# A graph layer with a routed expert layer: idle writes in the counting, a later attention, and a divided last piece

## The chip, the cores and the metric

The kernel runs on one core of a Trainium2 chip. The metric is the device time of one execution in microseconds (us); the time before is the median of three runs. Engines are named as in the profile: PE (TensorE; PEld its weight loads), DVE (VectorE), ACT (ScalarE), POOL (GpSimd) and SP, which issues most plain DMAs. GpSimd issues the indirect DMAs: gathers of rows by an index column, and scatters.

## The reference, cut to what matters

x is [128 graphs, 128 nodes, 256], adj is [128, 128, 128]; M = 16384 nodes.

```python
x = x + gnn(layernorm(x), adj)      # (1+eps) x + adj @ x, then a 256-512-256 MLP with relu
xn = layernorm(x)
h = xn @ W_gat                      # 16 values a node: 4 heads x 4 experts
# 1048576 edges (src, dst) and a loop on every node: softmax over the edges of each dst
e = leaky_relu(a_src[src] + a_dst[dst], 0.2)
alpha = softmax of e over the edges with the same dst
agg = segment_sum(h[src] * alpha, dst)
scores = layernorm(agg).mean over heads      # 4 scores a node
w, i = softmax(top_2(scores))
x = x + sum over the two chosen experts: w * (gelu(xn @ W1[i] + b1[i]) @ W2[i] + b2[i])
```

JAX clips or wraps edge indices, so edges whose source lies outside the range count too: they all take the last row, and only their number by destination matters. The kernel calls finding that number the counting.

## The kernel before, in words

**First stage (to about 680 us).** The graph layer runs tile by tile (32 tiles of four graphs); VectorE sorts the real edges beside it (`sort_edges`). Each node's 24 attention values go to `table` in DRAM, the normalized rows and the residual of the first 88 graphs to `xr`, the turned rows to `xn_d`.

**Second stage, in an order written out by a planner.** Class `Plan` holds lists of Python generators for three engines ("pool", "tensor", "vector"). A task issues some instructions and yields what they are thought to cost, or a condition: `plan.was(name)` waits until something is `done`, `plan.after(us)` until so much planned time is over. The planner always steps the engine that is free first, so these costs decide in which order the instructions of each engine stand. On the chip each engine runs its own list in that order and waits for real data.

- *Counting* (`count_edges`, class `Runs`, L489 to L773): a sorting network over 8192 int16 numbers a partition. A step is one VectorE instruction of at most 2048 pairs (`_cuts`, L509), with its cost yielded; `_pairs` is L496, `build` L520, `merge` L538, `push` L652. Then `histogram` (L700) counts with matmuls (L745, closed by L760): VectorE makes the operands (L727, L737), TensorE multiplies between its expert matmuls.
- *Gathers* (`Gathers.task`, L909, issued at L873): 13 blocks of 47 columns, each column one indirect DMA of 128 rows of `table` into `hs`; the last block is one plain load from `last`, which `last_block` (L985) packs. `pitch` (L899) is the planned time of one: 1.6 beside the counting, 1.33 after. Up to three blocks (and two of the blocks 3, 4, 8) may be ahead of attention. Rows asked for with `ask` (piece results `fin`, routed rows `r_x`, scatters at L880) go between them. A small copy `seen<-marks` (L864) ties GpSimd to TensorE's progress.
- *Attention* (`attend`, L1051): per block a segmented softmax by scans on VectorE (L1085 to L1140), with exponentials on ScalarE (L1121), and a store of running states. Ahead of it `spread` (L952) places destination values, and `last_block` waits for one gathered row `e` (L1030, L1032) and moves it by matmuls (L1041).
- *Pieces* (`pieces`, L2188): the graphs in seven pieces (ends 32, 52, 64, 82, 88, 106, 128); when the states of a piece are there, its ends are gathered (`fin`), and `finish_attention` and `gates` (L1154, L1218) make the weights.
- *Dense experts* (class `Experts`, L1547, L1566): for the last 40 graphs (tiles 22 to 31) all four experts are computed, 40 units, stored to `ys`, and added with their gates later (`stored`, L2245, additions at L2272) when the piece's gates are known. In the built program a unit is 8 L1547, 2 L1560 and 16 L1566; the profile counts each twice.
- *Routed experts* (`Routes`, `Routed`): the first 88 graphs are routed. After five pieces a list (`Routes.task`) sorts nodes into units of 256 nodes for one pair of experts; 47 units. A unit gathers its rows (`r_x`, two DMAs), is turned by TensorE (`turn`, L1693) and copied by ScalarE (L1697), multiplied (L1712, L1566), finished on VectorE (L1735 with the bias, L1745 with the result), and scattered to the output (L880). Seven row buffers: the rows of unit u + 7 are asked for when unit u has been scattered.

Of the kernel before, what the change touches and what calls it, by code (L numbers as in the profile page):

```python
# [13 lines left out]
F32 = mybir.dt.float32  # L14
# [11 lines left out]
P = 128  # L26
# [39 lines left out]
BARE_US = 6.95  # L66
TURN_US = 0.8
GATHER_US = 1.33
BESIDE_US = 1.6
LAND_US = 4.0  # L70
AHEAD_US = 6.0
SCALAR_US = 4.0
LOCK_US = 0.02
# [4 lines left out]
AHEAD = (3, 4, 8)  # L78
AHEAD_BUFS = 2
HIST_US = 2.0  # L80
SLACK_US = 20.0
PART = 3
YIELD_US = 16.0
# [10 lines left out]
    for start, (stop, a, b) in zip([0] + [g for g, _, _ in PARTS], PARTS)  # L94
]
PIECES = [slice(a, b) for a, b in zip(
    (0, 32, 52, 64, 82, 88, 106), (32, 52, 64, 82, 88, 106, 128)
)]
MOST = 32
EARLY = 4  # L100
# [388 lines left out]
class Runs:  # L489

    def __init__(self, nc, a, b, length, n):
        self.nc, self.pair, self.length, self.n = nc, Pair(a, b), length, n

    def _pairs(self, d):  # L496

        nc, s = self.nc, self.n // self.length
        v = self.pair.cur[:, 0 : self.n].rearrange("p (k t d) -> p k t d", t=2, d=d * s)
        o = self.pair.other[:, 0 : self.n].rearrange("p (k t d) -> p k t d", t=2, d=d * s)  # L500
        for t, op in enumerate((ALU.max, ALU.min)):
            for cols, cost in self._cuts(self.n // 2, d * s):
                nc.vector.tensor_tensor(
                    o[:, :, t, cols], v[:, :, 0, cols], v[:, :, 1, cols], op=op
                )
                yield cost
        self.pair.swap()

    def _cuts(self, n, inner):  # L509
# [10 lines left out]
    def build(self):  # L520

        nc, n, s = self.nc, self.n, self.n // self.length
        run = 1
        while run < self.length:
            v = self.pair.cur[:, 0:n].rearrange("p (k t l s) -> p k t l s", t=2, l=run, s=s)
            o = self.pair.other[:, 0:n].rearrange("p (k t l s) -> p k t l s", t=2, l=run, s=s)
            a, b = v[:, :, 0, :, :], v[:, :, 1, ::-1, :]
            for t, op in enumerate((ALU.max, ALU.min)):
                for cols, cost in self._cuts(n // 2, s):
                    nc.vector.tensor_tensor(  # L530
                        o[:, :, t, :, cols], a[..., cols], b[..., cols], op=op
                    )
                    yield cost
            self.pair.swap()
            yield from self._clean(run // 2)
            run *= 2

    def merge(self, keep_all):  # L538

        nc, n, s = self.nc, self.n, self.n // self.length  # L540
        v = self.pair.cur[:, 0:n].rearrange("p (l t s) -> p l t s", t=2, s=s // 2)
        a, b = v[:, :, 0, :], v[:, ::-1, 1, :]
        out = self.pair.other
        for at, op in ((0, ALU.max), (n // 2, ALU.min))[0 : 2 if keep_all else 1]:
            half = out[:, at : at + n // 2].rearrange("p (l s) -> p l s", s=s // 2)
            for cols, cost in self._cuts(n // 2, s // 2):
                nc.vector.tensor_tensor(half[:, :, cols], a[:, :, cols], b[:, :, cols], op=op)
                yield cost
        if keep_all:
            d = self.length // 2  # L550
            self.pair.swap()

            self.length *= 2
            yield from self._clean(d)
        else:
            self.n //= 2
            self.pair.swap()
            yield from self._clean(self.length // 2)
# [13 lines left out]
def count_edges(tc, nc, c, sp, dram):  # L572

    raw = [c.counted_raw] + [sp.tile([P, 4096], I32, name=f"raw{i}") for i in range(2)]
    pick = picks(nc, sp)
    runs = Runs(nc, c.counted, raw[1].bitcast(I16), 32, EC)
    yield from runs.build()
    yield from runs.merge(False)
    yield from runs.to_one()
    if runs.pair.cur is not c.counted:  # L580
        raw = [raw[1], raw[0], raw[2]]
    lst = runs.pair.cur[:, 0:CROW]
    col = c.col


    far_op, small = CROW / 960 + 0.15, CROW / 1920 + 0.15
    nz = raw[1][:, 0:CROW].bitcast(F32)
    nc.vector.tensor_single_scalar(nz, lst, 0.0, op=ALU.is_gt)
    yield small

    NONE = 2 * CROW * P
    empty = raw[0][:, CROW // 2 : CROW].bitcast(BF16)
    nc.vector.tensor_scalar(
        empty, lst, 0.0, float(NONE), op0=ALU.is_equal, op1=ALU.mult
    )
    yield small
    dst = raw[2][:, 0:CROW]
    nc.vector.tensor_scalar(dst, lst, -1.0, float(M), op0=ALU.mult, op1=ALU.add)
    yield small
    cbk = raw[2][:, CROW:]  # L600
    nc.vector.tensor_single_scalar(cbk, dst, 7, op=ALU.arith_shift_right)
    yield small
    nc.vector.tensor_single_scalar(dst, dst, P - 1, op=ALU.bitwise_and)
    yield small
    at = raw[1][:, CROW:].bitcast(F32)
    nc.vector.memset(at[:, 0:1], 0.0)
    for lo, hi in ((1, CROW // 2), (CROW // 2, CROW)):
        nc.vector.tensor_tensor(
            at[:, lo:hi], cbk[:, lo:hi], cbk[:, lo - 1 : hi - 1], op=ALU.not_equal
        )  # L610
        yield far_op / 2
    for v in halves(CROW):
        nc.vector.tensor_tensor(at[:, v], at[:, v], col[:, v], op=ALU.mult)
        yield far_op / 2
    first = raw[0][:, CROW:].bitcast(F32)
    for v in halves(CROW, 4):
        nc.vector.tensor_tensor_scan(
            first[:, v], at[:, v], at[:, v],
            first[:, v.start - 1 : v.start] if v.start else 0.0, op0=ALU.max, op1=ALU.max,
        )  # L620
        yield far_op / 2
    for v in halves(CROW):
        nc.vector.tensor_tensor(at[:, v], col[:, v], first[:, v], op=ALU.subtract)
        yield far_op / 2
    nc.vector.scalar_tensor_tensor(
        at, at, float(CKC), nz, op0=ALU.is_ge, op1=ALU.mult, accum_out=c.bad[:, 7:8]
    )
    yield far_op
    for v in halves(CROW):
        nc.vector.scalar_tensor_tensor(  # L630
            first[:, v], cbk[:, v], float(CKC), first[:, v], op0=ALU.mult, op1=ALU.subtract
        )
        yield far_op / 2
    low = dst.bitcast(F32)
    for v in halves(CROW):
        nc.vector.scalar_tensor_tensor(
            low[:, v], first[:, v], float(P), dst[:, v], op0=ALU.mult, op1=ALU.add
        )
        yield far_op / 2
    value, moved = raw[1], raw[2]  # L640
    for v in halves(CROW):
        nc.vector.tensor_tensor(value[:, v], low[:, v], empty[:, v], op=ALU.max)
        yield far_op / 2


    nc.vector.tensor_single_scalar(
        value[:, CROW:], value[:, 0:CROW], P * CROW, op=ALU.bitwise_xor
    )
    yield small
    w = P * CKC  # L650

    def push(value, moved, by, rate):  # L652
        for v in halves(w, 2 if rate == 1 else 1):
            nc.vector.tensor_single_scalar(
                moved[:, v], value[:, v], P * by, op=ALU.bitwise_xor
            )
            yield w / 1920 / 2 + 0.1
        for v in halves(w - by, 4 // rate):
            to = slice(v.start + by, v.stop + by)
            nc.vector.tensor_tensor(value[:, to], moved[:, v], value[:, to], op=ALU.min)  # L660
            yield (w - by) / 960 / 4 + 0.1

    by = CROW // 2
    while by >= P:
        yield from push(value, moved, by, 1)
        by //= 2
    both = raw[0].bitcast(I16)
    value, moved = both[:, 0:w], both[:, w:]
    for v in halves(w, 4):
        nc.vector.tensor_single_scalar(value[:, v], raw[1][:, v], P * P, op=ALU.min)  # L670
        yield w / 960 / 4
    while by:
        yield from push(value, moved, by, 2)
        by //= 2
    yield from histogram(nc, c, value, raw, pick, sp)
# [167 lines left out]
class Gathers:  # L843
# [53 lines left out]
        return pool.tile([P, CB, ROW], F32, name="hs")  # L897

    def pitch(self):  # L899
        return GATHER_US if "counts" in self.plan.at else BESIDE_US  # L900

    def ask(self, todo, name, how=None, soon=False):
# [82 lines left out]
def last_block(nc, c, plan, gathers, once, ps):  # L985
# [42 lines left out]
    gathers.ask([(row, gathers.table, source)], "last row")  # L1028
    yield 1.5
    yield plan.was("last row")  # L1030
    each = once.tile([P, CB * ROW], F32, name="room")
    nc.vector.tensor_tensor(  # L1032
        each.rearrange("p (c f) -> p c f", f=ROW),
# [17 lines left out]
def attend(nc, c, plan, gathers, states, dst_t, aw, once, ps, ahead):  # L1051
# [2 lines left out]
    dst_x = aw.tile([P, H, COLS], F32, name="dst_x")  # L1054
    nc.gpsimd.memset(dst_x[:, :, 0 : COLS - P], 0.0)
    yield from spread(nc, c, dst_t, dst_x, once)
    yield from last_block(nc, c, plan, gathers, once, ps)
    pre_ex = [once.tile([P, 2, H, CB + 1], F32, name=f"pre{i}") for i in range(2)]
    for t in pre_ex:
# [1 line left out]
    before = None  # L1061
    for k in range(NBL):
        if k >= EARLY:
            yield plan.was("counts")
        yield plan.was(f"block{k}")
        hs = gathers.rows.pop(k)
        cols = slice(k * CB, (k + 1) * CB)
# [702 lines left out]
def adj_ffn_kernel(  # L1770
# [352 lines left out]
    with tc.tile_pool(name="moe", bufs=2) as mp, tc.tile_pool(  # L2123
# [98 lines left out]
        def lists(routes):  # L2222
# [7 lines left out]
            for k, reach in enumerate(REACH):  # L2230
# [3 lines left out]
                experts.routed = routed  # L2234
                experts.ask()
                plan.done("listed", 5.0)
            plan.done("routes")

        def sums():
# [448 lines left out]
```

## Time and profile before

| what | value |
|---|---|
| runs | 2069.66, 2071.39, 2074.95 us; median 2071.39 |
| profiled execution, own time | 2072.77 us |
| its span (first to last instruction) | 2071.0 us |
| mean granted TensorE clock | 0.973 |
| PE busy | 1926.6 us, 93% |
| DVE busy | 1553.8 us, 75% |
| POOL busy | 1115.6 us, 54% |
| gathers `hs` (L873) | 564, mean 1.13 us |

How to read it: busy time is the union of an engine's instructions. Idle time is put down to what ended it, "issue" where nothing that the profile shows did. The waits list an engine and its line, what it waited for, the sum in us, how often, and the longest. A timeline row is start, length, engine, line, operation, output<-inputs and shape; equal neighbours are merged (x4).

### The profile page before, as it was taken

What the parts mean: (1) busy time and instruction counts of PE and PEld (TensorE: products, weight loads), DVE (VectorE), ACT (ScalarE), POOL (GpSimd) and SP (SyncE); (2) the same over time, 40 slices, a digit from 0 to 9 for tenths busy, and PEclk for the clock granted to TensorE, in tenths of its full rate; (3) what the DMA queues carried; (4) which work ended last, traced back from release to release, by engine and by line L of the source; (5) the groups of instructions that cost most, each with busy time, mean ns of one, the idle gap of its engine ahead of it and who ended that gap; (6) DMA issues with size and microseconds to landing.
All of it is one profiled execution on the core that took longest, in us unless ns stands there. A gap on an engine that the chain in (4) does not pass through costs nothing. (4 is left out here: it accounts for less than half of the span.)

```text
span 2071.0 us, 28612 instructions
## 1 busy us (share of the span) xinstructions
PE 1926.6 (93%) x8938; PEld 1443.0 (70%) x8938; DVE 1553.8 (75%) x4106; ACT 854.1 (41%) x1541; POOL 1115.6 (54%) x1064
## 2 busy tenths in 40 slices
PE   7999989889999799999999999999899999999894
PEld 4666767657666465666667666888788787788783
DVE  5889999858898797999983653747636856858576
ACT  5878544444443222333232433344334343335241
POOL 2111111111110688888877777777777767774723
PEclk9999999999999899999999999999999999999997
DMA  9888888697762121233213444444564355666955
GB/s 238 213 230 210 193 243 193 179 188 179 121 140 75 57 58 49 60 131 100 69 41 113 123 144 126 104 143 135 183 209 136 97 178 139 147 149 216 369 177 199
DMA packets 299157, 313.38 MB, mean 151 GB/s; under 512 B 111649, under 2 KB 239603, under 8 KB 298870
## 3 DMA queue, kind: packets, MB, share of 16 engines
q1 hardware_dynamic: 231382, 241.19, 36.8%
q0 software_dynamic: 67616, 70.28, 19.3%
q8 instruction: 75, 1.23, 0.2%
q14 instruction: 84, 0.69, 0.1%
HBM read 156.93 MB, written 130.32 MB: 139 GB/s over the span
## 5 line engine op out<-in xcount | busy, mean ns | idle before, releaser
L873 POOL DMA_INDIRECT hs<-table,index x564 | 637.6, 1130 | 165.1 <-issue 154.5
L1566 PE MATMUL big<-mw,m_hid 128*128 (+1 forms) x2784 | 626.2, 382 | 0.0
L1566 PEld LDWEIGHTS big<-mw,m_hid 128*128 128x128 f32 x2784 | 522.2, 190 | 84.6 <-issue 17.0
L1712 PE MATMUL m_phid<-m_xn,mw 128*128 128x256 f32 x1504 | 344.7, 386 | 27.9 <-ACT m_xn L1697 21.7
L1712 PEld LDWEIGHTS m_phid<-m_xn,mw 128*128 128x128 f32 x1504 | 285.8, 192 | 71.9 <-ACT m_xn L1697 26.0
L1573 ACT COPY m_out<-big 128x1024 f32<-128x1024 f32 x87 | 88.1, 1012 | 528.3 <-PE big L1566 522.5
L1547 PE MATMUL m_phid<-m_xn,mw 128*128 128x512 f32 x640 | 288.1, 601 | 10.6 <-issue 10.0
L1965 POOL DMA_DIRECT2D at<-in_adj_dram x31 | 41.4, 1334 | 433.7 <-DMA at<-self_eye 368.3
L2047 PE MATMUL big<-w_sb,hid 128*128 128x256 f32 x1024 | 237.9, 388 | 11.1 <-ACT h_t L2028 10.7
L2036 PE MATMUL p_hid<-h_t,w_sb 128*128 128x512 f32 x512 | 232.3, 604 | 9.6 <-ACT h_t L2028 7.2
L2047 PEld LDWEIGHTS big<-w_sb,hid 128*128 128x128 f32 x1024 | 194.3, 194 | 42.0 <-ACT h_t L2028 16.7
L1547 PEld LDWEIGHTS m_phid<-m_xn,mw 128*128 128x128 f32 x640 | 121.8, 192 | 145.3 <-issue 131.2
L1718 ACT ACTIVATE m_hid<-m_phid,r_b 128x256 f32<-128x256 f32 x376 | 155.9, 472 | 153.0 <-PE m_phid L1712 115.6
L2036 PEld LDWEIGHTS p_hid<-h_t,w_sb 128*128 128x128 f32 x512 | 94.7, 192 | 118.1 <-issue 97.8
L1551 ACT ACTIVATE m_hid<-m_phid,mb 128x512 f32<-128x512 f32 x160 | 108.7, 687 | 141.3 <-PE m_phid L1547 141.2
L873 POOL DMA_INDIRECT fin<-states,ends x128 | 142.9, 1116 | 37.5 <-issue 33.4
L1745 DVE SCALAR_TENSOR_TENSOR r_x<-m_out,r_x 128x256 f32<-128x256 f32 x188 | 87.1, 484 | 61.3 <-ACT m_out L1573 53.0
L880 POOL DMA_INDIRECT out_dram<-r_x,places x94 | 110.5, 1175 | 28.6 <-issue 12.3
L873 POOL DMA_INDIRECT r_x<-xr,nodes x94 | 99.9, 1063 | 36.6 <-issue 24.6
L2040 ACT ACTIVATE hid<-p_hid,b_sb 128x512 f32<-128x512 f32 x128 | 87.2, 682 | 77.1 <-PE p_hid L2036 77.1
L2019 POOL DMA_DIRECT2D xt<-b_sb x32 | 43.2, 1351 | 106.2 <-ACT xn L1903 63.5
L1735 DVE SCALAR_TENSOR_TENSOR r_x<-b_rows,r_x 128x256 f32<-128x256 f32 x188 | 87.2, 485 | 6.3 <-issue 2.2
(393 smaller groups left out, 2520.5 us busy)
## 6 DMA issues: line engine op xcount, KB each, us to landing
mw<-in_L_ffn_W_dram SPq DMA_DIRECT2D x102, 512.0 KB
states<-room SPq DMA_DIRECT2D x55, 564.0 KB
ys<-m_out SPq DMA_DIRECT2D x40, 512.0 KB
y_in<-ys SPq DMA_DIRECT2D x40, 512.0 KB
xt<-in_x_dram SPq DMA_DIRECT2D x32, 512.0 KB
xt<-b_sb POOLq DMA_DIRECT2D x32, 512.0 KB
x_d<-x SPq DMA_DIRECT2D x32, 512.0 KB
xn_d<-xn_t SPq DMA_DIRECT2D x32, 512.0 KB
```

What stands on the lines that cost most here:

```text
L873: self.nc.gpsimd.indirect_dma_start(out=out, out_offset=None, in_=rows, in_offset=bass.IndirectOffsetOnAxis(ap=index, axis=0),)
L880: sc = self.nc.gpsimd.indirect_dma_start(out=rows, out_offset=bass.IndirectOffsetOnAxis(ap=index, axis=0), in_=values, in_offset=None, bou ...
L1547: nc.tensor.matmul(p_hid, w1[:, k, f * P : (f + 1) * P], xn[:, k, :], start=(k == 0), stop=(k == 1),)
L1551: nc.scalar.activation(hid[:, f, :], p_hid, AF.Gelu, bias=b1[:, f : f + 1])
L1566: nc.tensor.matmul(p_y[:, s, :], hid[:, f, s * P : (s + 1) * P], w2[s // 2][:, f, :], start=(f == 0 and not b2), stop=(f == DH // P - 1 an ...
L1573: nc.scalar.copy(y, p_y)
L1712: nc.tensor.matmul(p_hid[:, half], w1[i][:, k, f * P : (f + 1) * P], xt[:, k, :], start=(k == 0), stop=(k == 1),)
L1718: nc.scalar.activation(hid[:, f, half], p_hid[:, half], AF.Gelu, bias=b1[i][:, f : f + 1])
L1735: self.nc.vector.scalar_tensor_tensor(x[:, s, D : 2 * D], b2[i], x[:, s, 2 * D + i : 2 * D + i + 1], x[:, s, D : 2 * D], op0=ALU.mult, op1 ...
L2036: nc.tensor.matmul(p_hid, w1_sb[:, k, f * P : (f + 1) * P], h_t[:, k, :], start=(k == 0), stop=(k == 1),)
L2040: nc.scalar.activation(hid[:, f, :], p_hid, AF.Relu, bias=b1_sb[:, f : f + 1])
L2047: nc.tensor.matmul(p_y[:, s, :], hid[:, f, s * P : (s + 1) * P], w2_sb[:, f, :], start=(f == 0), stop=(f == DH // P - 1),)
```

## The change

Behind every counting step whose planned cost is at least 1.0, VectorE writes zeros over 230 float32 numbers of a tile `pad` that nobody reads (`rest`); 156 such writes are built. Attention blocks from number 4 (the fifth) on wait for the first list, and no longer for the counting. The last piece (graphs 106 to 128) is two, 106 to 117 and 117 to 128. The work behind the gathered row `e` in `last_block` comes 20 planned us later. The planned pitch of a gather is 1.8 until `spread` is over, then 1.36 beside the counting instead of 1.6; since the planner orders by these costs, the order on every engine of the second stage changes with them.

```diff
-BESIDE_US = 1.6
+SPREAD_US = 1.8
+BESIDE_US = 1.36
+LAST_US = 20.0
+REST = 230
+REST_US = 0.11
 PIECES = [slice(a, b) for a, b in zip(
-    (0, 32, 52, 64, 82, 88, 106), (32, 52, 64, 82, 88, 106, 128)
+    (0, 32, 52, 64, 82, 88, 106, 117), (32, 52, 64, 82, 88, 106, 117, 128)
 )]
...
+    def rest(self, cost):
+        if cost < 1.0:
+            return cost
+        self.nc.vector.memset(self.pad, 0.0)
+        return cost + REST_US
...   (in _pairs, build and merge)
-                yield cost
+                yield self.rest(cost)
...   (count_edges)
+    pad = sp.tile([P, REST], F32, name="pad")
...   (push)
-            yield w / 1920 / 2 + 0.1
+            yield runs.rest(w / 1920 / 2 + 0.1)
-            yield (w - by) / 960 / 4 + 0.1
+            yield runs.rest((w - by) / 960 / 4 + 0.1)
...   (pitch)
+        if "spread" not in self.plan.at:
+            return SPREAD_US
...   (last_block)
     yield plan.was("last row")
+    yield plan.after(LAST_US)
...   (attend)
     yield from spread(nc, c, dst_t, dst_x, once)
+    plan.done("spread")
...
         if k >= EARLY:
-            yield plan.was("counts")
+            yield plan.was("first list")
...   (lists, after each list)
                 plan.done("listed", 5.0)
+                plan.done("first list")
```

More of the change, by code (lines that the diff above doesn't have):

```diff
@@ L489, with __init__ @@
 class Runs:
-    def __init__(self, nc, a, b, length, n):
+    def __init__(self, nc, a, b, length, n, pad):
         self.nc, self.pair, self.length, self.n = nc, Pair(a, b), length, n
+        self.pad = pad
+    def rest(self, cost):
[3 more added lines that the diff above has]
+        return cost + REST_US
     def _pairs(self, d):
@@ L532, in build @@
                     )
-                    yield cost
+                    yield self.rest(cost)
             self.pair.swap()
@@ L547, in merge @@
                 nc.vector.tensor_tensor(half[:, :, cols], a[:, :, cols], b[:, :, cols], op=op)
-                yield cost
+                yield self.rest(cost)
         if keep_all:
@@ L575, in count_edges @@
     pick = picks(nc, sp)
-    runs = Runs(nc, c.counted, raw[1].bitcast(I16), 32, EC)
+    pad = sp.tile([P, REST], F32, name="pad")
+    runs = Runs(nc, c.counted, raw[1].bitcast(I16), 32, EC, pad)
     yield from runs.build()
```

## The prediction

> **What bounds the kernel now.** I read the page first, then the granted clock and busy time in stretches of 100 us, then the waits of TensorE, then the timelines of single engines where these pointed. The first 680 us (graph layer, edge sort) are the same instructions in both programs except for eight idle writes near the end, so only the rest matters.
>
> ```profile
> span 2071.0 us, 28612 instructions
> PE 1926.6 (93%) x8938; PEld 1443.0 (70%) x8938; DVE 1553.8 (75%) x4106; ACT 854.1 (41%) x1541; POOL 1115.6 (54%) x1064
> ```
>
> TensorE is busy nearly throughout, so time can come only from its holes and from what follows its last matmul. The timeline of the end (start, length, both in us; the bracket is the idle time before):
>
> ```profile
> 2040.08 1.01 ACT L1573 COPY m_out<-big 128x1024 f32<-128x1024 f32 x1 [5.85 <-issue]
> 2041.12 1.92 DVE L1745 SCALAR_TENSOR_TENSOR r_x<-m_out,r_x 128x256 f32<-128x256 f32 x4
> 2042.96 15.92 DVE L2272 SCALAR_TENSOR_TENSOR acc<-y_in,gate,acc 128x256 f32<-128x256 f32 x40
> 2046.58 13.15 POOL L880 DMA_INDIRECT out_dram<-r_x,places  x1 [0.30 <-DVE acc L2272]
> ```
>
> TensorE's last row there is 13.98 us from 2026.02, so it ends at 2040.0. Then 10 of the 40 dense additions (L2272, four instructions each) still stand on VectorE until 2058.9, and the last scatter of GpSimd, which needs 1.0 to 1.3 us elsewhere, lies under them for 13.15 us. It ends at 2059.74, and the closing takes 11.3 us more. The waits of TensorE (us in total, times, longest):
>
> ```profile
> PE big L1693 <- DMA r_x<-xr,nodes: 8.7, 5, 3.1
> PE pt L1041 <- DVE room L1032: 2.9, 1, 2.9
> PE big L745 <- DVE counted L737: 2.6, 1, 2.6
> ```
>
> and, on VectorE, the wait behind the second of these:
>
> ```profile
> DVE room L1032 <- DMA e<-table,e: 16.4, 1, 16.4
> ```
>
> The r_x line is the important one: routed rows come through GpSimd, which issues 881 indirect transfers. An undisturbed one takes 0.95 us and 0.30 of issue, 1.26 in all, which reads as 76% busy: the stretches from 700 to 1800 show 73 to 84%, so GpSimd is full there. Beside the counting it is slower. Two rows of its timeline, both beside 2048-wide L503 steps (1.22 us each):
>
> ```profile
> 818.86 0.95 POOL L873 DMA_INDIRECT hs<-table,index  x1 [0.30 <-issue]
> 821.37 1.97 POOL L873 DMA_INDIRECT hs<-table,index  x1 [0.30 <-issue]
> ```
>
> Some gathers meet the seam between two steps and pass, others wait a whole step. Adding up both timelines from 684.5 to 1116.3: the stretches of long steps hold 106 gathers in 192.2 us, 1.81 each. Outside them: 17 in 33.7 us (spread), 89 in 139.6 us (attention, 1024-wide steps, other counting), 51 in 69.9 us (histogram, 1.37).
>
> **The change, part by part.**
>
> *The idle writes: cost.* 156 memsets of 230 numbers, all ahead of the histogram. No such row exists. The nearest:
>
> ```profile
> L1060 DVE MEMSET pre<- x2: 378/378/378, 859.4 to 859.8; 128x384 f32 x2
> L452 DVE MEMSET shifts<- x1: 165/165/165, 4.7 to 4.7; 128x128 int32 x1
> ```
>
> The slope is 0.83 ns a number, so 230 last 0.25 us. The two L1060 start 0.41 apart and the next instruction 0.33 behind; less 154 numbers (0.13), a memset moves its successor by 0.20 to 0.28. Below: L1074 and L1075 (62 ns each) start within 12 ns of their successors, so nearly nothing. Range 0.02 to 0.28; I take 0.20, since 230 is nearest 384. That is 31 us of VectorE.
>
> *Who pays.* TensorE meets the histogram in its own order. The first L745 comes two dense units (14.5 us each by the starts of L1547, 1007.97 and 1022.48) later in the new program; without the L1041 wait TensorE reaches it at 1035.3 + 29.0 - 2.9 = 1061.4. VectorE was ready at 1035.2. New: -16.4 (L1032 now comes 20 us of planned work later, and its gather is long done), +10.3 (a fourth attention block now stands ahead; the third took 920.0 to 926.3 and 933.5 to 937.4), -4.3 (L503 steps start 1.136 apart, 1.164 on average with gathers; I let that excess go), + 156 x 0.20 = 31.2: 1056.0. That is ahead of TensorE, so the memsets cost nothing and both waits, 2.9 and 2.6, go: **-5.5**. At 0.28 the cover is gone and TensorE stalls 7 us. What is late next is GpSimd.
>
> *The idle writes: gain, and the new place of the routed rows.* In the built order, the r_x gathers of the eighth routed unit (the first asked for behind a scatter) are number 467 of GpSimd's transfers now and 508 after: 41 attention gathers moved ahead of them. Now that unit is issued at 1393.8, 1.6 us ahead of its transposes. The counting ends at 1116.3 + 19.0 (8 more L1547, 24 more L1566 and 4 bias products of the program ahead of L760) - 5.5 = 1130. Until then 156 gathers fit outside the long stretches (17 + 89 + 50). The long stretches are 151 x 1.336 = 202 us. At what pitch? Floor 1.26 (VectorE idle), ceiling 1.81 (no effect). One window per step of 1.336, and a marks copy (0.35) every tenth gather or so: I take 1.35, so 150; 306 in all. The other 202 take 1.347 each (206 took 277.5 us between 1116.3 and 1393.8), so number 508 is out at 1402, and the transposes go at 1403.6. TensorE would be there at 1395.3 - 5.5 + 7.1 (one first half now ahead of them) = 1396.9: a new wait of **+6.7**, part of which the present r_x waits (8.7) already hold, so **+5**. With the ends: 1.26 gives 316 and no wait, 1.81 gives 268 and 58 us.
>
> The Trainium skill ("SBUF — State Buffer", section "Who interferes with whom") speaks against this gain: it holds, marked as inferred, that a tensor_tensor takes only the read side of the port that VectorE and GpSimd share, while descriptor generation needs the write side. By that the 141 memsets behind a tensor_tensor would win GpSimd nothing and the sum would go by the 1.81 end; the 1.97 us row beside L503 says that gathers do wait for such a step. The same section lets a trn2 VectorE instruction with at most one SBUF input pass GpSimd freely, by which each memset is an open window; no run so far shows a gather beside one.
>
> *Attention from block five behind the first list.* The first list stands behind four attention blocks, not five, so it is earlier by one block (10 us). TensorE gains nothing: dense work lasts until 1298 and the first routed rows are issued 71.8 us ahead of use. Behind the wait stand only attention's own steps, with the gathers prefetched.
>
> *Last piece divided.* 55 more small VectorE instructions of 0.2 to 0.5 us, some 15 us, two ACT table loads (1.28 each) and one 11-graph load more, all beside matmuls: nothing. The gates now close behind routed units 30, 36 and 39 of 47 instead of 33 and 43. So the additions, which wait for gates, start at unit 30 and all 40 stand ahead of the last three units.
>
> *Tail.* With nothing behind L1745, the last scatter takes 1.0 to 1.3 at 2046.6 and ends near 2047.7, not 2059.7: **-12.0**. It cannot be more unless the closing shrinks; less if y_in is late.
>
> *Turns.* The order where transposes stand right ahead of a first half, with a 1.24 us hole (ACT's copy), occurs 20 times instead of 18: **+2.5**.
>
> Sum: 2071.0 - 5.5 + 5 - 12.0 + 2.5 = 2061.0, and the execution's own time lies 1.8 above its span, 2062.8. The median shown is 1.4 below that execution's 2072.77, so 2061.4; I give **2060**.
>
> **Rivals.** (1) *The windows do not serve GpSimd*: slower. Gathers stay near 1.81 and every routed unit waits for rows 41 places later. At 1.81 that is 58 us instead of 6.7: about 2110. Break-even at 8 gathers fewer (10 us): a pitch of 202 / 142 = 1.42; clearly slower from 12 fewer, 1.46. For: only estimates stand behind 1.35. Against: steps of 0.16 to 0.3 us beside L737 and L1474 leave medians of 1.26 to 1.29. (2) *The memsets open GpSimd fully*: 1.26, no row waits, and the present 8.7 shrink too: about 2047. (3) *Dear memsets or crossed loads*: memsets at 0.28 (+7), or y_in loads, now spread over units 30 to 44, holding up the weights of a routed unit as at 1956 (4.18 wait, then 32 matmuls in 11.1 instead of 7.1 us while the clock is low): +8. About 2070, no change.
>
> **How the numbers follow.** Forecast (2050 to 2066) 0.46; rival 2, 0.17; rival 3, 0.17; rival 1, 0.20. About 0.3% (6.2 us) is what a measurement of this kernel can tell from no change. Forecast and rival 2 are faster but for the upper edge: 0.61. Rival 3 and that edge: 0.18. Rival 1, most of it, and double mishaps: 0.21. The range runs from 2043 (rival 2 with fewer row waits) to 2088 (rival 1 at 1.57: 129 gathers, 28 us).
>
> **What would show it.** No L2272 behind the last L1745 and a last scatter near 1 us; no L1032 wait; no L745 wait on L737 above 3 us; gathers beside long steps about 1.35 apart; the eighth unit's rows issued near 1402; TensorE's end near 2042. Wrong if TensorE waits for r_x by more than 20 us in sum, or if the last scatter is still late.

## The result, and the profile after

| | before | after |
|---|---|---|
| median | 2073.77 us (10 runs, 2069.66 to 2079.19) | 2080.48 us (10 runs, 2076.74 to 2089.92) |
| ratio of the runs | | 1.0040, 95% interval 1.0026 to 1.0054 |
| profiled execution, own time | 2072.77 us | 2079.75 us |
| its span | 2071.0 us | 2077.8 us |

The change makes the kernel slower by 0.4%, where the forecast was faster by 0.5%. Line numbers below are those of the changed kernel (before in brackets where it helps). The page's first lines answer to those shown of before:

```profile
span 2077.8 us, 28822 instructions
PE 1925.7 (93%) x8938; PEld 1445.4 (70%) x8938; DVE 1585.5 (76%) x4317; ACT 857.0 (41%) x1545; POOL 1085.3 (52%) x1064
```

TensorE's work is the same within 1 us, VectorE has 32 us more (the writes and the divided piece) and GpSimd 30 us less. So the difference lies in holes again. The end (start, length, engine, line; bracket: the idle time before and what ended it):

```profile
2046.55 13.98 PE L1583 MATMUL big<-mw,m_hid 128*128 x64
2061.66 1.93 DVE L1762 SCALAR_TENSOR_TENSOR r_x<-m_out,r_x 128x256 f32<-128x256 f32 x4 [3.20 <-ACT m_out L1590]
2066.80 0.98 POOL L893 DMA_INDIRECT out_dram<-r_x,places  x1 [0.30 <-issue]
```

Nothing stands behind the last L1762, and the last scatter takes 0.98 us instead of 13.15. TensorE's last matmul ends at 2060.5 and the span 17.3 us later, 31.0 before. But TensorE itself ends 20.5 us later than before. Its waits (total, times, longest) say where:

```profile
PE m_phid L1729 <- ACT m_xn L1714: 27.6, 24, 1.3
PE m_phid L1564 <- ACT m_hid L1568: 22.7, 2, 22.1
PE big L1710 <- DMA r_x<-xr,nodes: 9.8, 4, 3.8
PE big L758 <- DVE counted L750: 3.4, 1, 3.4
```

The second row is new: one hole of 22.1 us, in the middle of the last dense unit. Its chain, read from the timelines of four engines:

```profile
1299.53 0.95 POOL L886 DMA_INDIRECT fin<-states,ends  x1 [0.30 <-issue]
1302.29 0.24 DVE L1193 TENSOR_TENSOR last<-fin,empty 128x80 f32<-128x80 f32 x1 [35.76 <-DMA fin<-states,ends]
1303.35 0.40 ACT L1205 ACTIVATE each<-each 128x240 f32<-128x240 f32 x1 [22.34 <-DVE each L1200]
1305.81 3.78 PE L1564 MATMUL m_phid<-m_xn,mw 128*128 128x512 f32 x4 [22.09 <-ACT m_hid L1568]
```

The second piece's 20 end rows (`fin`) leave GpSimd until 1299.5. VectorE has waited 35.8 us for them, ScalarE 22.3 us with the exponential L1205 at the head of its list, and behind L1205 stand the dense units' own activations (L1568), for which TensorE waits. Before, VectorE had the same rows at 1258.99 and the exponential ran with no idle time ahead of it:

```profile
1271.47 0.40 ACT L1188 ACTIVATE each<-each 128x240 f32<-128x240 f32 x1
```

GpSimd was full all that time and came to each place late: item 508, the eighth unit's rows, is issued at 1426.1; I had 1402. Of my signs of being wrong none appeared (the r_x waits are 9.8 us, below 20, and the last scatter is short): I had looked for the loss at r_x alone.

The histogram's wait (3.4) has to do with GpSimd too. On VectorE, between the first gather and the histogram, the longest wait is one for gathered rows, in the attention that stands ahead of the histogram:

```profile
DVE e L1110 <- DMA hs<-table,index: 8.4, 1, 8.4
```

### The profile page after: what moved, and what is told of

It reads as the page before. It is cut to its first block, busy times and chain, and to the rows that moved or that the text cites. A ratio compares the mean times of both kernels' runs of the same rounds, so it can differ in the third digit from the quotient of the medians.

```text
span 2077.8 us, 28822 instructions
## 1 busy us (share of the span) xinstructions
PE 1925.7 (93%) x8938; PEld 1445.4 (70%) x8938; DVE 1585.5 (76%) x4317; ACT 857.0 (41%) x1545; POOL 1085.3 (52%) x1064
## 3 DMA queue, kind: packets, MB, share of 16 engines
q0 software_dynamic: 67616, 70.28, 19.1%
## 5 line engine op out<-in xcount | busy, mean ns | idle before, releaser
L886 POOL DMA_INDIRECT hs<-table,index x564 | 617.6, 1095 | 165.1 <-issue 157.5
L1583 PE MATMUL big<-mw,m_hid 128*128 (+1 forms) x2784 | 629.8, 384 | 0.0
L1583 PEld LDWEIGHTS big<-mw,m_hid 128*128 128x128 f32 x2784 | 526.8, 192 | 86.0 <-issue 17.4
L1729 PE MATMUL m_phid<-m_xn,mw 128*128 128x256 f32 x1504 | 340.8, 383 | 27.6 <-ACT m_xn L1714 27.6
L1568 ACT ACTIVATE m_hid<-m_phid,mb 128x512 f32<-128x512 f32 x160 | 108.7, 687 | 136.2 <-PE m_phid L1564 136.1
L1762 DVE SCALAR_TENSOR_TENSOR r_x<-m_out,r_x 128x256 f32<-128x256 f32 x188 | 87.0, 483 | 59.1 <-ACT m_out L1590 48.7
L893 POOL DMA_INDIRECT out_dram<-r_x,places x94 | 99.5, 1058 | 30.4 <-issue 10.5
L877 POOL COPY seen<-marks 128x1 f32<-128x1 f32 x87 | 31.2, 359 | 123.4 <-ACT marks L882 123.1
```

Of the source, the lines that this page charges most:

```text
L886: self.nc.gpsimd.indirect_dma_start(out=out, out_offset=None, in_=rows, in_offset=bass.IndirectOffsetOnAxis(ap=index, axis=0),)
L893: sc = self.nc.gpsimd.indirect_dma_start(out=rows, out_offset=bass.IndirectOffsetOnAxis(ap=index, axis=0), in_=values, in_offset=None, bou ...
L1568: nc.scalar.activation(hid[:, f, :], p_hid, AF.Gelu, bias=b1[:, f : f + 1])
L1583: nc.tensor.matmul(p_y[:, s, :], hid[:, f, s * P : (s + 1) * P], w2[s // 2][:, f, :], start=(f == 0 and not b2), stop=(f == DH // P - 1 an ...
L1729: nc.tensor.matmul(p_hid[:, half], w1[i][:, k, f * P : (f + 1) * P], xt[:, k, :], start=(k == 0), stop=(k == 1),)
L1762: self.nc.vector.scalar_tensor_tensor(x[:, s, D : 2 * D], y[:, 2 * i + s, :], x[:, s, 2 * D + i : 2 * D + i + 1], x[:, s, D : 2 * D], op0= ...
```

## Why GpSimd was late

Beside the sorting steps the writes do what they were put there for. GpSimd, then VectorE, in one stretch:

```profile
819.97 1.02 POOL L886 DMA_INDIRECT hs<-table,index  x1 [0.30 <-issue]
821.29 1.02 POOL L886 DMA_INDIRECT hs<-table,index  x1 [0.30 <-issue]
822.62 1.02 POOL L886 DMA_INDIRECT hs<-table,index  x1 [0.30 <-issue]
823.64 0.55 POOL L877 COPY seen<-marks 128x1 f32<-128x1 f32 x1
824.34 1.97 POOL L886 DMA_INDIRECT hs<-table,index  x1 [0.16 <-issue]
826.62 1.00 POOL L886 DMA_INDIRECT hs<-table,index  x1 [0.30 <-issue]
```
```profile
821.49 0.25 DVE L505 MEMSET pad<- 128x230 f32 x1
821.66 1.16 DVE L515 TENSOR_TENSOR raw<-counted 128x2048 int16<-128x2048 int16 x1
822.82 0.25 DVE L505 MEMSET pad<- 128x230 f32 x1
```

A write moves VectorE by 0.17 us (821.49 to 821.66), a step and its write take 1.325, and exactly one gather passes per step: starts 1.32 apart, better than my 1.35. But a copy `seen<-marks` (L877) makes the gather behind it miss its window: 822.62 to 826.62 is 4.00 us for two gathers, where two steps are 2.65. A copy costs 1.35 us there; I had counted 0.35. And in the loops of `push` (L667, L673) the pitch is another:

```profile
1037.04 1.64 POOL L886 DMA_INDIRECT hs<-table,index  x1 [0.30 <-issue]
1038.99 1.71 POOL L886 DMA_INDIRECT hs<-table,index  x1 [0.30 <-issue]
```
```profile
1037.23 0.25 DVE L505 MEMSET pad<- 128x230 f32 x1
1037.40 1.16 DVE L667 TENSOR_SCALAR raw<-raw 128x4096 int16<-128x4096 int16 x1
1038.56 0.25 DVE L505 MEMSET pad<- 128x230 f32 x1
1038.73 1.16 DVE L673 TENSOR_TENSOR raw<-raw 128x2040 int16<-128x2040 int16 x1
1039.88 0.25 DVE L505 MEMSET pad<- 128x230 f32 x1
1040.05 1.16 DVE L673 TENSOR_TENSOR raw<-raw 128x2040 int16<-128x2040 int16 x1
```

The gather of 1037.04 starts 0.19 ahead of the write at 1037.23, as those beside L515 do, and yet ends only at 1038.68, 0.12 after L667. The next one, begun in L673, waits for the write at 1039.88 and ends 0.82 later, in the middle of the next L673. So a gather is held twice: soon after its start by a two-input step (L515, L673), until a write or a seam, and again some 0.7 us later by a one-input step (L667), to that step's end. This is read from the rows; no run isolates it. The Trainium skill ("SBUF — State Buffer", section "Who interferes with whom") has both halves: a two-input VectorE instruction contends with a GpSimd instruction that reads SBUF, and one in a 2-port mode, which tensor_scalar can enter, holds the port pair that both engines share for its whole length, so that GpSimd is blocked. The rows fit both, though the gather of 1037.04 starts ahead of L667 and is held by it all the same. They do not fit the inferred remark that I cited in the prediction: the gather of 824.34 lasts 1.97 us beside two tensor_tensor steps, where undisturbed ones last 0.95, and the writes behind such steps do gain time. In the prediction I weighed only what the section says of tensor_tensor and of memsets.

Adding up both timelines from the first gather on, the sorting stretches of more than 4 us hold 94 gathers in 139.6 us (1.49) and the `push` loops 28 in 51.8 (1.85): 122 in 191.4 us, 1.57 each. Before it was 69 in 126.1 (1.83) and 25 in 50.9 (2.03). With the short stretches of one or two steps the changed kernel has 129 in 202.6 us; I had 150 in 202. (The recorded expectations below use 1.64, 122 in 200.6 us, which takes in 9.2 us of sorting ahead of the first gather.) A gather for each step of 1.325 would be 105 beside the sorting; 8 copies stand there.

## The experiments

The first four ran on one chip, where the kernel before took 2072.4 us (median of 26 runs). Their theories: A, GpSimd is late until about item 508 and TensorE pays for that lateness wherever it next waits; B, only the place of the exponential on ScalarE costs.

**e1_no_writes.** The order kept, no write issued.

```diff
-        self.nc.vector.memset(self.pad, 0.0)
         return cost + REST_US
```

> The changed kernel with its order of instructions on every engine, but the 156 idle writes are not issued. Theory A (GpSimd is late until about item 508 and TensorE pays for it, at whatever place it next waits; the writes do speed it up beside the sorting): beside long steps the gathers fall back from 1.64 us each (122 in 200.6 us) to about 2.0 (90 in 179 us); in the 21 us that VectorE saves 17 more fit outside, so GpSimd is some 15 gathers or 19 us later at item 508 (1426.1 -> 1445), and the holes of TensorE behind it, 22.1 + 9.8 us, grow to about 51. The 3.4 us wait for the histogram goes. About 2080 + 19 - 3 = 2096. Rival (the writes gain GpSimd nothing and only cost VectorE 26 us): item 508 is not later than 1426, the time is 2077 or less.

Measured: 2094.78 us, ratio to before 1.0111 (1.0080 to 1.0142). Item 508 is issued 760.7 us after the first gather instead of 742.4, 18 later (expected 19). Its waits of TensorE:

```profile
PE m_phid L1563 <- ACT m_hid L1567: 31.4, 2, 30.8
PE big L757 <- DVE counted L749: 14.0, 1, 14.0
```

The size came out, one place did not: the histogram's wait grew to 14.0 although VectorE had 26 us less to do, because attention blocks that wait for gathers stand ahead of the histogram on VectorE (there the wait of 8.4 us is 24.7). So GpSimd's lateness reaches TensorE there too. The new order alone, with the divided piece, costs 22 us; the writes give 14 of them back. Which part of the order costs them no run separates.

**e2_push_bare.** No writes in `push`, the others kept (`bare` returns the same planned cost).

```diff
-            yield runs.rest(w / 1920 / 2 + 0.1)
+            yield runs.bare(w / 1920 / 2 + 0.1)
...
-            yield runs.rest((w - by) / 960 / 4 + 0.1)
+            yield runs.bare((w - by) / 960 / 4 + 0.1)
```

> The changed kernel in the same order, but the 41 idle writes behind the steps of push (L667, L673) are left out; the 115 behind the sorting steps (L515, L542, L559) stay. Theory A with its finer reading of the trace: behind a tensor_scalar step (L667) a window serves nothing, in the push loops two gathers pass per three steps with or without writes, so the writes only stretch these loops by 41 x 0.165 = 7 us. Then GpSimd comes to item 508 about 7 us earlier (1419), the hole of 22.1 us shrinks to 15, and the histogram's wait (3.4) goes: about 2070. Rival (a write serves one gather everywhere): the loops lose some 8 gathers, 10 us, less the 7 us saved: item 508 at about 1429, 2080 to 2084.

Measured: 2079.66 us, 1.0044 (1.0028 to 1.0060), as the changed kernel. Item 508 stands at 744.3 us after the first gather, not earlier. The loops hold 23 gathers in 49.7 us without writes (2.16) and 28 in 51.8 with them (1.85). My expectation (2070) was wrong and the time is the rival's: a write in `push` helps less than beside the sorting, but it pays for itself.

**e3_exp_later.** The second piece's exponential ordered later.

```diff
-    yield plan.after(2.0)
+    yield plan.after(25.0 if name == "fin1" else 2.0)
     nc.scalar.activation(each, each, AF.Exp)
```

> The changed kernel, but the exponential of the second piece's finish (ScalarE, L1205 the second time) is ordered 23 us of planned work later, behind the next first half. Theory A: the hole of 22.1 us in which TensorE waits for m_hid behind that exponential goes, but TensorE then comes to the eighth unit's rows 22 us earlier, which are still issued at about 1426, so its wait for r_x grows from 9.8 to about 30: 2080, within 4. Theory B (the price is ScalarE's order: an exponential put ahead of its data; GpSimd's lateness costs nothing elsewhere): r_x waits stay near 10 and the time falls by 22 to about 2058.

Measured: 2082.21 us, 1.0054 (1.0035 to 1.0073). The waits:

```profile
PE pt L1391 <- DVE each L1387: 21.9, 1, 21.9
PE big L1710 <- DMA r_x<-xr,nodes: 19.1, 9, 9.7
```

The hole behind L1205 is gone and the time is not: 21.9 us have moved to a small matmul of the next list (L1391), which waits for the same piece, and the r_x waits grew to 19.1. (The profile is of the slowest execution, 2087.83 us; in it the histogram's wait is 10.0 and one gather lasts 10.32 us.) Theory B falls; A had the time right and only half of the place.

**e4_no_copies.** No copies `seen<-marks` until the counting is over.

```diff
     def wait(self):
+        if "counts" not in self.plan.at:
+            return
```

> The changed kernel in the same order, but GpSimd's small copies seen<-marks (L877), which tie it to TensorE's progress, are left out until the counting is over (21 of 87 copies). Beside the sorting each copy makes the gather behind it miss its window: two gathers in 4.0 us instead of 2.65, 1.35 us a copy. Theory A: GpSimd comes to item 508 about 20 x 1.35 = 27 us earlier (1399), the 22.1 us hole and the r_x waits (9.8) shrink to 5 or less together: about 2053. Theory B (ScalarE's order alone): the piece's rows come earlier by as much, so the hole goes too, about 2058: this run doesn't tell A from B, but tells both from the rival that GpSimd's lateness has no part in the loss (2080) or that the copies hold back transfers that would otherwise get in the way of others (2080 or more).

Measured: 2057.95 us, 0.9954 (0.9927 to 0.9981), 22 under the changed kernel. Item 508 comes 723.1 us after the first gather, 19 earlier (27 earlier and a time of 2053 us were expected), and of the hole 6.7 us are left. The trace has 61 copies instead of 87, and in the same 139.6 us beside the sorting 101 gathers instead of 94:

```profile
PE big L1712 <- DMA r_x<-xr,nodes: 9.8, 5, 5.7
PE m_phid L1566 <- ACT m_hid L1570: 8.1, 2, 6.7
```

With e1 and e3 this shows that the time follows GpSimd's lateness, though not one for one: 18 us more or 19 us less of it are 14 us more or 22 us less in the time.

The other fourteen runs fell on chips where the kernel before takes 2320 to 2349 us, so they are compared with it only there. The changed kernel on one of these is its t0_after, 1.0003 (0.9976 to 1.0031).

**e6, r6, s6: the last piece undivided.**

```diff
-    (0, 32, 52, 64, 82, 88, 106, 117), (32, 52, 64, 82, 88, 106, 117, 128)
+    (0, 32, 52, 64, 82, 88, 106), (32, 52, 64, 82, 88, 106, 128)
```

> The changed kernel, but the last piece (graphs 106 to 128) is one again. Theory A (the tail comes from the new planned pitch 1.36, which puts everything that waits for gathers earlier in VectorE's order, and not from the division): no L2290 stands behind the last L1762, TensorE's last matmul and the span's end lie 17 us apart as in the changed kernel, and the time is that of the changed kernel, 2080 within 3. Rival (my prediction's reading: the division frees the gates and with them the additions): the additions come back behind the last L1762 and the last scatter is late again by 12: about 2092.

> The kernel of e6_undivided again (the changed kernel with the last piece one again), because the chip of e6 ran the kernel before in 2337 us, with TensorE waiting for its own instructions, and can't be set beside the others. As there: theory A (the tail comes from the order that the new planned pitch makes, not from the division): 2080 within 3, no L2290 behind the last L1762. Rival (the division makes the tail): 2092, additions and a late scatter at the end.

> The kernel of e6 and r6 (the changed kernel with the last piece one again), for a chip that can be set beside the first four runs. Theory A: 2080 within 3, the span ends 17 us after TensorE's last matmul (it was 17.1 in r6). Rival: 2092.

> The changed kernel itself, as the control beside the others of its chip. Where the kernel before takes 2072: 1.004 again (2080). Where it takes 2320 to 2340: the same as s6 and r6 (the changed kernel with the last piece undivided), 1.000 to 1.002 of the kernel before, if the division is worth nothing; 0.995 if it is worth the 12 us that the prediction gave it.

Measured: 1.0003, 1.0003 and 1.0022, with the divided kernel at 1.0003. The end in r6:

```profile
2283.11 13.98 PE L1583 MATMUL big<-mw,m_hid 128*128 x64
2298.21 1.92 DVE L1762 SCALAR_TENSOR_TENSOR r_x<-m_out,r_x 128x256 f32<-128x256 f32 x4 [3.19 <-ACT m_out L1590]
2303.37 0.98 POOL L893 DMA_INDIRECT out_dram<-r_x,places  x1 [0.30 <-DVEq L2313]
```

No additions at the end, and the span (2314.2) ends 17.1 us after TensorE; in e6 and s6 it is 17.0. The 12 us that I gave the division (0.5%) are not there, and nothing above the 0.3% that these runs can tell; the shorter end comes from the rest of the new order. I take the planned pitch for it, since with 1.6 in place of 1.36 in the changed kernel 22 additions are built behind the last L1762; that was not run.

**e7, r7, s7, t7: the writes alone, in the order before** (memset at the same steps, planned costs unchanged).

```diff
+        if cost >= 1.0:
+            self.nc.vector.memset(self.pad, 0.0)
+        return cost
```

> The kernel before in its own order, with the 156 idle writes added and nothing else. Theory (a write moves VectorE by 0.165 us; two more dense units ahead of the histogram are what covers them in the changed kernel): VectorE comes to the histogram 156 x 0.165 = 26 us later, TensorE, which was there 0.1 us after VectorE, waits some 25 us for L737 instead of 2.6; GpSimd gains about 15 gathers (19 us) ahead of 1060, the r_x wait of 8.7 goes. 2071 + 23 - 9 = 2085 (2080 to 2092). Rival (the writes are what made the changed kernel slower, by themselves and in any order): slower by as much or more, but with r_x waits above 10. Rival (the writes are a gain and only the new order spoils it): below 2071.

> The kernel of e7_before_writes again (the kernel before with the 156 idle writes and nothing else). Theory: VectorE comes to the histogram 26 us later, TensorE waits some 25 us for L737 instead of 2.6, the r_x wait of 8.7 goes: 2085 (2080 to 2092). Rival (the writes slow the kernel by themselves in any order, through GpSimd): slower with r_x waits above 10. Rival (the writes are a gain and only the new order spoils it): below 2071.

> The kernel of e7 and r7 (the kernel before with the 156 idle writes and nothing else), for a chip that can be set beside the first four runs. Theory: VectorE comes to the histogram 26 us later, TensorE waits some 25 us for L737 instead of 2.6, the r_x wait of 8.7 goes: 2085 (2080 to 2092). Rival (a gain that only the new order spoils): below 2071.

> The kernel of e7, r7 and s7 (the kernel before with the 156 idle writes and nothing else). Where the chip runs the kernel before in 2072: TensorE waits some 25 us for L737 at the histogram instead of 2.6, the r_x wait of 8.7 goes: 2085 (2080 to 2092). Rival (a gain that only the new order spoils): below 2071. Where it takes 2320 to 2340: as the kernel before, as in the three tries.

Measured: 0.9972, 0.9982, 0.9993, 0.9967 (intervals some 0.5% wide, two of them reach 1). The expected 2085 would be 1.0065, above all four intervals. The 25 us at the histogram did not come: TensorE's wait ahead of its first matmul there was 5.6 to 8.8 us in the four profiles. VectorE reached it in t7 at 1035.9 (1030.1 in the kernel before, on its chip), though it had made 26 us of writes: the 16.4 us that it stood waiting for the gathered row (L1032) in the kernel before are not there in t7, so there most of the writes seem to have gone into that idle time. In s7 the row is waited for (14.0 us) and VectorE comes at 1050.1, and TensorE, late itself, still waits only 5.6. No profile of the kernel before exists for these chips. What the writes alone do on the faster chips stays open.

**s10_counts.** Attention waits for the counting again.

```diff
-            yield plan.was("first list")
+            yield plan.was("counts")
```

> The changed kernel with one part undone: attention from block five waits for the counting again, not for the first list. In the built order the eighth routed unit's rows are then GpSimd's transfer 495 instead of 508 and the second piece's ends stand 6 places earlier. Theory A (every place on GpSimd ahead of what TensorE next waits for costs 1.27 us, so this part of the change has a price, where the prediction gave it none): the hole of 22.1 us shrinks by 6 x 1.27 = 8, the r_x wait does not grow since its rows come 13 x 1.27 = 16 us earlier: 2080 - 8 = 2072 (2068 to 2075). Rival (the part costs nothing, as predicted): 2080.

Measured: 1.0056 (1.0024 to 1.0088), beside 1.0003 for the changed kernel: no gain from undoing it. Whether it is a loss stays open, since the intervals overlap and the two ran on different chips. The price of 8 us that I looked for is not shown.

**e5, r5, e8, e9, s11: copies left out.** e5 and r5: the edit of e4 in the kernel before. e8: no copy at all. e9: e4 with more writes. s11: s10 with every third copy while counting.

```diff
-        if n > self.waited:
+        if n >= self.waited + (1 if "counts" in self.plan.at else 3):
```

> The kernel before in its own order, with GpSimd's copies seen<-marks left out until the counting is over (as in e4_no_copies). Theory A (TensorE pays for GpSimd's lateness, and only as far as it shows as a wait): the kernel before waits 8.7 us for r_x and 2.9 for the gathered row's products; a copy costs GpSimd some 0.5 to 1 us there, 23 copies, 10 to 20 us in all, so these waits nearly go: 2071 - 8 = 2063 (2060 to 2066). Then the change's order without the copies (2058) is ahead of the order before without them by only about 5, of which the tail gives 13. Rival (the copies matter only beside the idle writes, where each makes a gather miss its window): nothing, 2072.

> The kernel of e5_before_no_copies again (the kernel before without the copies seen<-marks until the counting is over). Theory A (TensorE pays for GpSimd's lateness only as far as it shows as a wait): the r_x waits (8.7) and the products' wait (2.9) nearly go: 2063 (2060 to 2066). Rival (the copies cost much only beside the idle writes): 2072.

> The changed kernel in the same order, with none of the 87 copies seen<-marks on GpSimd. Between the counting's end and item 508 there are some 20 of them at 0.35 us each, 7 us. Theory A: of the 16.5 us that TensorE still waits behind GpSimd in e4_no_copies (6.7 for the piece's exponential, 9.8 for r_x) 7 go: about 2051. Rival (GpSimd would only wait elsewhere, for row buffers and scattered units, so late copies cost nothing): 2058, as e4_no_copies.

> e4_no_copies, and the idle write also behind the 14 long f32 steps that make the list of sorted edges (L620 to L657 there, some 1.22 us each, with gathers of 1.4 to 2.2 us beside them), with the planned costs unchanged, so in the same order. Theory A: in that stretch (945 to 980) a gather passes per step, about 5 more gathers in 37 us, 6 us, less 2 us of VectorE: GpSimd is 4 us earlier and of the 16.5 us that TensorE still waits behind it 4 go: 2054 beside 2058 for e4. Rival (a gather beside those steps is held by their writes too, as beside L667, and a window serves nothing): 2058 to 2060.

> s10_counts, and while the counting lasts only every third copy seen<-marks is issued (7 instead of 21), in the same order: the tie to TensorE stays, looser. Theory A: 14 copies at 1.35 us each and the order's 8: the lateness of 32 us falls to about 5: 2055 where the chip runs the kernel before in 2072. Where it takes 2320 to 2340, the copies are a brake that e5, e8 and e9 lacked: within 1% of the kernel before there. Rival (any copy left out is a loss or nothing): 2072 or more.

Measured: 1.0138, 1.0195, 1.149, 1.051, 1.034, all slower, where each was expected faster or, for s11, within 1%. In the changed kernel it is the more the fewer copies are left: 87 (1.0003), 69 (s11), 61 (e9), none (e8). In e8 (VectorE, ScalarE, GpSimd, then TensorE):

```profile
976.36 0.55 DVE L1062 COPY room<-pt 128x376 f32<-128x376 f32 x1 [150.27 <-remote]
967.82 1.01 ACT L1591 COPY m_out<-big 128x1024 f32<-128x1024 f32 x1 [93.11 <-remote]
957.94 0.95 POOL L887 DMA_INDIRECT hs<-table,index  x1 [0.30 <-issue]
917.41 0.79 PE L1058 MATMUL pt<-room,e 128*128 128x376 f32 x1 [1.79 <-issue]
920.21 0.79 PE L1058 MATMUL pt<-room,e 128*128 128x376 f32 x1 [2.02 <-issue]
```

From 826 to 958 GpSimd issues a gather every 1.26 us without a break; VectorE does nothing for 150 us and ScalarE for 93, and they go on 17 and 9 us after the last gather. "remote" means that the profile has no releaser for the wait, but the rows say what was read: VectorE's copy takes `pt`, and TensorE's last matmul into it (L1058) ended at 921.0, 55 us before the copy starts. TensorE itself starts single matmuls 2.80 us apart there, with "issue" ahead of each. So while GpSimd issues without a break, TensorE hardly proceeds and its finished product is taken up late; why is not shown. On these chips leaving copies out costs time. e4, the one version that beat both kernels, was not run on them; its nearest relative e9 (e4 with 14 more writes) takes 1.051 there, so I would not carry it on.

## Why the prediction was wrong, step by step

| step | forecast | the two profiles |
|---|---|---|
| tail | -12.0 | 31.0 to 17.3: -13.7 |
| waits of L1041 and the histogram | -5.5 | the first gone (-2.9), the second 2.6 to 3.4: -2.1 |
| rows from GpSimd | +5 | r_x 8.7 to 9.8, and the new hole of 22.1: +23.2 |
| turns | +2.5 | 18 holes of 21.7 to 24 of 27.6: +5.9 |
| weights late (rival 3: +8) | 0 | 6.2 to none: -6.2 |
| sum | -10 | +7.1 (spans: +6.8) |

- *The failed step* is the idle writes' gain, "At what pitch? ... I take 1.35, so 150". It was 1.57 and 129. I took one window per step for every step and 0.35 us for a copy. The rows show 1.35 us for a copy beside a sorting step, and `push` at 1.85. By the end of the counting (1129.3; 1130 forecast) 287 gathers were out, not 306, and item 508 came 24 us later than forecast.
- *The base of that step* was a little off as well: in the kernel before 97 gathers start in 181.8 us of long steps, 1.87 each, not 106 in 192.2 (1.81).
- *Its consequence was followed to one place only.* Item 508 had "+6.7" by r_x waits, and for a pitch of 1.57 the text gave 28 us over the forecast, the upper end of its range (2088). The pitch came, and the row of the table is +23.2 instead of +5. But most of it showed at the second piece's ends, through VectorE and ScalarE; I had costed the later attention and the pieces at nothing and had not asked which exponential stands ahead of whose activation. Rival 1, which had a chance of 0.20, is what happened, at 1.57 instead of its 1.81; its reason holds only in part, since beside the sorting steps the windows do serve GpSimd. The break-even of 1.42 was named.
- *The writes' cost* was right: 0.17 us each (0.20 taken), 26 us in all. But VectorE's first part of the histogram was ready at 1062.2 and not at 1056.0, since I had put the waits of the attention ahead of it at nothing: 8.4 us for gathered rows and 3.3 for ScalarE. TensorE came at 1058.8, not 1061.4, and waited 3.4. Without the 8.4 us VectorE would have been ready near 1053.8 (an estimate), so the two dense units do cover the writes.
- *The tail* was right in size; its cause was read wrongly: not the division (r6).
- *Turns and weights* were off by 3 and 6 us in opposite directions and cancel in part, which is luck.
- The measured 2080 lies in the range (2043 to 2088); the sign was on the other side.

## What to carry to other kernels

When a change speeds up a full engine by opening windows, look at every kind of instruction that will stand beside it and at everything else that the engine does in that stretch: here a quarter of the steps stood in loops that blocked it in another way, and a copy of 0.35 us cost a whole step. And follow a late engine to every in-order queue that it feeds: the loss shows at the first of them, here an exponential at the head of ScalarE's list, and moving that instruction moves the hole, not the time. A small tie between engines whose removal gains time on one chip can be worth time on another: try its removal on more than one chip.

## What the runs showed that I had not expected

- The windows can lock in step: beside sorting steps gathers start 1.32 us apart, one per step, for as long as nothing disturbs them; without writes the mean there was 1.83. But they can be missed in a row: in e3, with the same instructions, one gather lasted 10.32 us beside eight writes.
- Chips differ: the same kernel takes 2072 us on one and 2320 to 2349 on others. There TensorE waits for its own "issue" within groups of matmuls (50.2 us at L1583 and 43.8 at L758 in the changed kernel, none listed on the first chip), and the mean granted clock is 0.93 instead of 0.97. In that run, too, some single matmuls start 2.80 us apart (1108.63, 1111.43, 1114.23).
